# Products of ones in TensorE's order in the first layer, and a second plan of expert tiles that is made in steps

## The chip, the cores and the metric

The kernel runs on one core of a Trainium2 chip. A core has TensorE (PE) for matmuls, VectorE (DVE), ScalarE (ACT) and GpSimd (POOL) for everything else, and SyncE (SP), which here only starts transfers. Each engine works through its own list of instructions in order, and waits on semaphores where it needs another's result. The metric is the time of one execution on the device, in microseconds, as the median of several runs.

## What is computed

Four sequences of 256 tokens with 256 features pass through two layers. Cut to what matters:

```
x = x + L0_attention(layernorm(x))   # 16 heads of 16, each token sees the last 128 (and itself)
x = x + L0_ffn(layernorm(x))         # 1024 wide, ReLU, weights stored in 4 bits with a scale for 64,
                                     # plus a low-rank (LoRA) part
x = x + L1_scan(layernorm(x))        # selective state space, 16 states:
                                     #   h[l] = exp(dt*A)*h[l-1] + dt*B[l]*x[l];  y[l] = sum_n C[l,n]*h[l,n]
n = layernorm(x)
a = n + L1_attention(rmsnorm(n))     # 32 query heads of 128, 4 key/value heads, causal
x = x + a + MoE(rmsnorm(a))          # 32 experts, each token goes to its 8 best, and a shared expert
```

The experts are chosen by sigmoid scores with a bias, and weighted by the scores of the eight, normalised. Everything is float32.

## The kernel before

**First layer, a sequence at a time.** `l0_attention(b)` is a generator. It projects q, k and v, then for eight pairs of heads `l0_lowest` (matmul L360) makes raw scores `l_sc` with matmuls of 16 rows (the head's dimension), and DVE reduces each head's scores to the lowest value per query (custom operation at L367, output `l_junk` and a column of `qpad`). That column makes a 17th row of q, so that a second product, `l_sT` in `l0_softmax` (L381), comes out transposed and with the lowest score taken off already. ACT takes the exponential (L388), POOL masks it (L393, L397), and `l0_values` (L409) multiplies by v, with matmuls that fill 32 columns of the array for each head (`l_av`). After every eight heads `l0_divide` copies the sums (ACT, L418, `l_o`), spreads the denominators over the partitions with a matmul (`l_den`, L420), inverts them on DVE (L421) and multiplies (L422, `l_oT`). `l0_close` (L430) applies the output weights (`l_po`, 16 matmuls on all 128x128 of the array) and DVE adds the result to x (L434). `feed_forward` then makes the norm (`ff_ln`, `ff_xn`), transposes (`ff_pT`, L190), and runs `ff_pu` (L482, up) and `ff_pd` (L497, down). While sequence 0 is in `l0_lowest`, `dequantise` unpacks the 4-bit weights on DVE (L238, L241, L245, L250) and adds the low-rank product that PE makes (`lora_up`, L240; `lora_dn`, L249).

**Scan.** `scan(b)` works through 16 states. For each one, PE copies B and C to all partitions (`sm_pbc`, L561, bf16, 96 rows), ACT makes the decay (L568), DVE multiplies (L572), scans (L574) and multiplies again (L579, `sm_hc`), and POOL adds up `sm_y` (L581). At the end PE transposes `sm_y` (`sm_py`, L587) and DVE adds it to x (L590).

**Second layer.** The attention runs in pairs of query heads (queries L655, scores L677/L678, values L727, output `at_po` L737). During the opening, SP also fills the DRAM areas of the expert stage with zeros (`zeros()`, 36 transfers, L752). The expert stage sorts the tokens by expert into slots of DRAM: `route` (L860 on) scores the tokens of a sequence, finds each token's slots (`mo_tops` L908, `mo_at` L909) and POOL scatters the rows with indirect transfers (`slots`, L918). A plan says which expert and which slots each tile of 128 slots takes. `plan("early")` makes the first 16 tiles (EARLY) from the first three sequences' counts, and `plan("late")` all others once the last sequence is routed. In it `late_pc` (L785) is a matmul with the counts, then follow some 20 small steps on DVE (L791 to L826), three matmuls `late_pv` that spread the results (L831), and the copies out of them (L836 to L851). `experts` is a software pipeline over the tiles: load a tile (SP, L1215), transpose (`mx_pT`, L1225), gate and up (`mx_pgu`, L1233), weights and slots (`mx_wj`, `at`, DVE, L1248, L1253, L1255), activation (`mx_act`, L1263), turn and down (L1268 to L1278), copy out (`mx_o`, L1286) and add into DRAM with an indirect transfer of POOL (`sum`, L1287). 64 tiles (FEWEST) are always there; a Switch on a count that the late plan leaves (`arm`, L844) picks the program for the rest. At the end four partial sums are loaded and added to x (L1366, L1371, L1372).

**Order.** The streams are Python generators. `play` takes from the stream with the smallest mark, `timed` gives each stream its marks as pieces `(from, to, steps)`, and so the instructions get the order in which they are handed over; a scheduler may still move them, except in the last `play(streams)` and in the Switch, which stand in a manual schedule. The late plan is the stream `planned()` (L1331), which makes the whole plan in one step, at (6, 6, 2).

**PSUM.** `ps(name)` hands out a bank of 128x512 f32. Tag "w" has six banks that go round, "acc" two. Whoever gets a bank waits until all readers of its last owner are done.

Of the kernel before, what the change touches and what calls it, by code (L numbers as in the profile page):

```python
# [16 lines left out]
P = 128  # L17
# [35 lines left out]
def block_kernel(ctx: ExitStack, tc, out, a):  # L53
# [16 lines left out]
    def g2(name, dtype=F32):  # L70

        return gen.tile([P, 512], dtype, tag="g2", name=name)

    def halves(t):
        return t.rearrange("p (t d) -> p t d", t=2)
# [119 lines left out]
    def rows(b):  # L195

        return x[:, 2 * b : 2 * b + 2, :]
# [154 lines left out]
    def l0_lowest(b, u, seq):  # L352

        pair, j = l0_pair(u)
        qT, kT = seq["qT"], seq["kT"]
        scs = [ps(f"l0_sc{b}_{h}") for h, _ in pair]
        for q, cols in ((0, slice(0, P)), (1, slice(P, 3 * P))):
            for (h, r0), sc in zip(pair, scs):
                rows_ = slice(r0, r0 + HD0)
                T.matmul(  # L360
                    sc[:, cols], qT[rows_, j, q * P : (q + 1) * P],
                    kT[rows_, j, 0 : cols.stop - cols.start], start=True, stop=True,
                )
        for (h, _), sc in zip(pair, scs):
            junk = l0.tile([P, 3 * P], F32, tag="junk", name=f"l0_junk{b}_{h}", bufs=1)
            for t, cols, mask in ((0, slice(0, P), mask_first), (1, slice(P, 3 * P), mask_window)):
                V.tensor_tensor_reduce(  # L367
                    junk[:, cols], sc[:, cols], mask, 1.0, 3.0e38,
                    ALU.add, ALU.min, seq["pads"][t][:, h, HD0 : HD0 + 1],
                )  # L370
# [54 lines left out]
    def l0_close(b, seq):  # L425

        po = halves(ps(f"l0_po{b}"))
        for t in range(2):
            for j in range(4):
                T.matmul(  # L430
                    po[:, t, :], seq[j // 2][:, j % 2, t * P : (t + 1) * P], wo0[:, j, :],
                    start=j == 0, stop=j == 3,
                )
        V.tensor_tensor(rows(b), rows(b), po, ALU.add)  # L434

    def l0_attention(b):

# [68 lines left out]
    def scan(b):  # L506
# [50 lines left out]
        for n in range(NS):  # L557
            pbc = halves(ps(f"sm_pbc{b}_{n}"))
            for i in range(2):
                k = i * NS + n  # L560
                T.matmul(  # L561
                    pbc[:, i, :], sel[:, k : k + 1].to_broadcast([96, P]), bc,
                    start=True, stop=True,
                )

            da = decays[n % 3]
            for c in range(2):
                A.activation(  # L568
                    da[:, c, 1:], dt[:, c, 1:], AF.Exp, scale=na[:, c, n : n + 1]
                )  # L570
            w = sw.tile([P, 2, S], F32, tag="w", name=f"sm_w{b}_{n}")
            V.tensor_tensor(w, u, pbc[:, 0:1, :].to_broadcast([P, 2, S]), ALU.mult)  # L572
            hs = sw.tile([P, 2, S], F32, tag="hs", name=f"sm_h{b}_{n}")
            V.tensor_tensor_scan(  # L574
                hs.rearrange("p c l -> p (c l)"), da.rearrange("p c l -> p (c l)"),
                w.rearrange("p c l -> p (c l)"), 0.0, ALU.mult, ALU.add,
            )
            hc = y if n == 0 else sw.tile([P, 2, S], F32, tag="hc", name=f"sm_hc{b}_{n}", bufs=2)
            V.tensor_tensor(hc, hs, pbc[:, 1:2, :].to_broadcast([P, 2, S]), ALU.mult)  # L579
            if n > 0:  # L580
                G.tensor_tensor(y, y, hc, ALU.add)  # L581
            yield
        yield
        py = halves(ps(f"sm_py{b}"))
# [189 lines left out]
    def plan(nm, n, early):  # L774

        def small(name, n=NE, dtype=F32):
            return end[0].tile([P, n], dtype, tag=f"plan_{name}", name=f"{nm}_{name}", bufs=1)

        c16 = stat.tile([P, NE], BF16, tag="mo_chosen16", name=f"{nm}_c16", bufs=1)
        V.tensor_copy(c16, chosen)
        pc = ps(f"{nm}_pc")[:, 0:NE]

        T.matmul(pc, ones16, c16, start=True, stop=True)  # L785
        count, tiles, cum, junk = small("count"), small("tiles"), small("cum"), small("junk")
        ti = small("ti", dtype=I32)
        ex, one = small("ex", 1), small("one")
        total = small("total", 1)
        j, used, vals = small("j", 1), small("used", 1), small("vals", 3)  # L790
        V.tensor_copy(count, pc)  # L791
        V.tensor_scalar(ti, count, 0.0 if early else float(P - 1), None, ALU.add)
        V.tensor_scalar(ti, ti, 7, None, ALU.arith_shift_right)
        V.tensor_copy(tiles, ti)
        if not early:
            V.tensor_tensor(tiles, tiles, taken, ALU.subtract)
        V.tensor_tensor_scan(cum, ones_ne, tiles, 0.0, ALU.mult, ALU.add)
        V.tensor_copy(total, cum[:, NE - 1 :])
        V.tensor_scalar(junk, cum, part, None, ALU.is_le)
        V.tensor_reduce(ex, junk, AX.X, ALU.add)  # L800
        V.tensor_scalar(one, enum, ex, None, ALU.is_equal)
        V.tensor_tensor(cum, cum, tiles, ALU.subtract)
        if early:

            V.tensor_scalar(taken, cum, -1.0, float(EARLY), ALU.mult, ALU.add)
            V.tensor_scalar(taken, taken, 0.0, None, ALU.max)
            V.tensor_tensor(taken, taken, tiles, ALU.min)
        else:
            V.tensor_tensor(cum, cum, taken, ALU.subtract)

        V.tensor_tensor(junk, one, cum, ALU.mult)
        V.tensor_reduce(j, junk, AX.X, ALU.add)
        V.tensor_tensor(j, part, j, ALU.subtract)
        V.tensor_scalar(j, j, float(P), None, ALU.mult)
        if early:
            V.tensor_copy(vals[:, 1:2], ex)
            V.scalar_tensor_tensor(vals[:, 0:1], ex, float(CAP), j, ALU.mult, ALU.add)
        else:
            live = small("live", 1)
            V.tensor_tensor(junk, one, count, ALU.mult)  # L820
            V.tensor_reduce(used, junk, AX.X, ALU.add)
            V.tensor_scalar(live, ex, float(NE) - 0.5, None, ALU.is_lt)
            V.tensor_tensor(vals[:, 1:2], ex, live, ALU.mult)
            V.tensor_tensor(vals[:, 2:3], used, j, ALU.subtract)
            V.scalar_tensor_tensor(j, ex, float(CAP), j, ALU.mult, ALU.add)
            V.tensor_tensor(vals[:, 0:1], j, live, ALU.mult)  # L826

        rows_of = 2 if early else 3
        pv = ps(f"{nm}_pv")[:, 0 : rows_of * n].rearrange("p (q i) -> p q i", q=rows_of)
        for q in range(rows_of):  # L830
            T.matmul(  # L831
                pv[:, q, :], vals[:, q : q + 1].to_broadcast([P, P]), ident[:, 0:n],
                start=True, stop=True,
            )
        which = end[0].tile([P, n], F32, tag=f"{nm}_which", name=f"{nm}_which", bufs=1)
        V.tensor_copy(which, pv[:, 1, :])  # L836
        regs = end[0].tile([1, 2, n], I32, tag=f"{nm}_regs", name=f"{nm}_regs", bufs=1)
        V.tensor_copy(regs[:, 0, :], pv[0:1, 0, :])
        V.tensor_scalar(regs[:, 1, :], pv[0:1, 1, :], 2.0 * P, None, ALU.mult)
        if early:  # L840
            return regs, which, None, None, None

        arm = end[0].tile([1, 1], I32, tag="arm", name="arm", bufs=1)
        V.tensor_scalar(arm, total[0:1], float(EARLY - FEWEST), None, ALU.add)  # L844

        lo = end[0].tile([P, n], F32, tag="lo", name="lo", bufs=1)
        hi = end[0].tile([P, n], F32, tag="hi", name="hi", bufs=1)
        spare = small("spare", 1)
        V.tensor_scalar(spare, part, float(CAP), None, ALU.add)
        V.tensor_scalar(lo, pv[:, 2, :], part, spare, ALU.is_le, ALU.mult)  # L850
        V.tensor_scalar(hi, lo, float(CAP - 1), None, ALU.max)  # L851
        return regs, which, lo, hi, arm

    taken = stat.tile([P, NE], F32, tag="taken", name="taken", bufs=1)

# [4 lines left out]
    def route(b, row):  # L860
# [51 lines left out]
            )  # L912

        if b == B - 2:
            tables.append(plan("early", EARLY, True))
        for t in range(2):
            for k in range(TOPK):
                inst = G.indirect_dma_start(  # L918
# [58 lines left out]
    def timed(stream, *pieces):  # L977


        marks = [lo + (hi - lo) * i / n for lo, hi, n in pieces for i in range(n)]  # L980
        return [stream, marks, 0, False]
# [346 lines left out]
            yield  # L1328


    def planned():  # L1331
        yield
        tables.append(plan("late", LATE, False))
        yield

    under_way = ahead, {}, {}, {}, {}, {}, {}, {}
    streams = [
        timed(shared(), (-1, 3, 2), (10, 18, 4)),
        timed(experts(FEWEST, range(FEWEST), under_way), (-2, FEWEST - 2, FEWEST)),
        timed(planned(), (6, 6, 2)),  # L1340
    ]
    play([timed(last_route[0], (0, 3, 3), (3, 5, 9))], streams)
    with tc.manual_schedule():
# [137 lines left out]
```

## Time and profile before

| | us |
|---|---|
| median of 3 runs | 1109.64 (1108.83 to 1111.13) |
| the profiled execution | 1098.13 |
| its span, first to last instruction | 1096.4 |
| mean granted TensorE clock | 0.908 |
| PE busy | 932.8 (85%) |
| DVE busy | 727.3 (66%) |
| POOL busy | 510.1 (47%) |
| ACT busy | 491.1 (45%) |

The profiled execution is 11.5 us shorter than the median of the runs, so the two are not mixed: differences between stages are read within the profile, and only their sum is carried over to the median. The times in the texts are from the start of the span. PE's clock ("PEclk") is the share of full speed that the throttle granted; it takes two values, 0.50 and 1.00, and a figure between them is a mean. A line of the timeline gives the start, the duration, engine, line, operation, out<-in, the shape, how many instructions were merged, and in brackets the idle time ahead of them with what ended it. A line of the windows gives a stretch, its length, and for each engine the busy time with the number of instructions, then the clock, the share of the DMA engines that was busy, and what they moved in GB/s. An f32 matmul appears as two records, so that x8 in a line of l_sc is four products.

The page's chain of work that ended last names the indirect sums (5%) and waits of PE in the expert stage first; the rest of the span falls into many small pieces, so the stages are read one by one.

### The profile page before, as it was taken

To read this page: it belongs to the slowest core of one execution; us is meant where nothing else is said; L and a number is where in the kernel's file an instruction comes from. 1 tells how busy PE (TensorE), PEld (TensorE's weight loads), DVE (VectorE), ACT (ScalarE), POOL (GpSimd) and SP (SyncE) were. 2 spreads that over 40 slices of the span, in tenths; PEclk is the share of its full clock that TensorE was granted. 3 is DMA by queue.
4 is the path that set the end of the run, shared out by engine and by line. 5 is a ranking of instruction groups with operands and counts; after the bars stand their busy time and mean duration, and the time that the engine had idled before them with its cause. 6 is when DMAs were issued, how large, how long until landed. Compare 5 with 4: busy or idle time off the path is not lost. (4 is left out here: it accounts for less than half of the span.)

```text
span 1096.4 us, 15761 instructions
## 1 busy us (share of the span) xinstructions
PE 932.8 (85%) x4589; PEld 696.5 (64%) x4589; DVE 727.3 (66%) x2237; ACT 491.1 (45%) x1503; POOL 510.1 (47%) x534
## 2 busy tenths in 40 slices
PE   4898976478898999999899989899998997999770
PEld 2655743355666687767677766677877875777650
DVE  6746149947996775899686489896475536555454
ACT  2031233324655364656555466655564554444330
POOL 5030123413456332344865135775335624888781
PEclk9576776788898999999999989999999998999995
DMA  8985999960110111111222473223223327799867
GB/s 214 236 180 132 255 246 241 245 217 26 39 49 30 39 39 38 49 49 49 62 80 71 134 226 101 72 99 101 68 83 99 108 84 252 147 155 150 155 73 206
DMA packets 131716, 134.31 MB, mean 123 GB/s; under 512 B 10592, under 2 KB 125440, under 8 KB 131616
## 3 DMA queue, kind: packets, MB, share of 16 engines
q1 hardware_dynamic: 118032, 114.12, 39.0%
q0 software_dynamic: 13584, 19.05, 9.6%
q8 instruction: 40, 0.66, 0.3%
q14 instruction: 60, 0.49, 0.1%
HBM read 70.45 MB, written 62.69 MB: 121 GB/s over the span
## 5 line engine op out<-in xcount | busy, mean ns | idle before, releaser
L607 POOL TENSOR_TENSOR at_q_rot<-at_q_t,at_q_t 128x512 f32<-128x512 f32 x64 | 85.0, 1328 | 139.6 <-DVE at_q_t L603 116.8
L686 ACT ACTIVATE at_pr<-at_pr,at_low 128x128 f32<-128x128 f32 (+1 forms) x256 | 113.6, 445 | 52.0 <-DVE at_low L682 49.7
L737 PE MATMUL at_po<-at_wo,at_oT 128*128 128x256 f32 x512 | 129.6, 387 | 2.2 <-ACT at_oT L730 2.1
L655 PE MATMUL at_pq<-at_hT,at_wq 128*128 128x256 f32 x512 | 125.7, 389 | 3.1 <-DVE at_q_t L603 1.8
L696 POOL TENSOR_SCALAR at_pr<-at_pr,at_rden 128x128 f32<-128x128 f32 x128 | 87.8, 695 | 80.4 <-DVE at_rden L691 62.9
L1287 POOL DMA_INDIRECT sum<-mx_o,at x73 | 113.8, 1559 | 24.1 <-issue 9.4
L581 POOL TENSOR_TENSOR sm_y<-sm_y,sm_hc 128x512 f32<-128x512 f32 x60 | 77.2, 1287 | 86.0 <-DVE sm_hc L579 82.9
L655 PEld LDWEIGHTS at_pq<-at_hT,at_wq 128*128 128x128 f32 x512 | 98.0, 196 | 19.7 <-DVE at_q_t L603 2.0
L737 PEld LDWEIGHTS at_po<-at_wo,at_oT 128*128 128x128 f32 x512 | 95.4, 193 | 17.3 <-ACT at_oT L730 3.4
L603 DVE TENSOR_TENSOR at_q_t<-at_pq,rope 64x512 f32<-64x512 f32 x128 | 88.1, 688 | 15.4 <-POOL at_k_rot L607 12.9
L568 ACT ACTIVATE decay<-sm_dt,na 128x255 f32<-128x255 f32 x128 | 58.7, 500 | 64.4 <-DVE sm_h L574 58.4
L574 DVE TENSOR_TENSOR_SCAN sm_h<-decay,sm_w 128x512 f32<-128x512 f32 x64 | 84.5, 1320 | 1.3
L719 ACT COPY at_pT<-at_pa 128x512 f32<-128x512 f32 x64 | 37.2, 581 | 104.1 <-PE at_pa L712 104.0
L918 POOL DMA_INDIRECT slots<-mo_row,mo_at x64 | 64.4, 1007 | 39.0 <-DVE mo_at L909 21.1
L682 DVE CUSTOM_DVE_ANT_0 at_pr<-at_sc,masks 128x128 f32<-128x128 f32 (+1 forms) x256 | 78.4, 353 | 4.6 <-PE at_sc L678 3.0
L678 PE MATMUL at_sc<-at_k_rot,at_q_rot 128*128 128x256 f32 x256 | 76.5, 380 | 0.0
L727 PE MATMUL at_pav<-at_pT,at_v 128*128 128x512 f32 x128 | 67.4, 609 | 2.8 <-DVE sm_hc L579 1.3
L601 DVE TENSOR_TENSOR at_q_t<-at_pq,rope 128x512 f32<-128x512 f32 x64 | 43.8, 684 | 38.4 <-PE at_pq L655 38.0
L393 POOL TENSOR_SCALAR_AFFINE_SELECT l_pr<-l_pr 128x512 f32<-128x512 f32 x32 | 22.4, 700 | 97.7 <-ACT l_pr L388 97.7
L700 ACT ACTIVATE at_pr<-at_pr,at_rden 128x256 f32<-128x256 f32 x128 | 57.9, 501 | 8.2 <-DVE at_rden L691 8.0
L677 PEld LDWEIGHTS at_sc<-at_k_rot,at_q_rot 128*128 128x128 f32 x256 | 47.9, 190 | 12.7 <-issue 2.7
L1233 PE MATMUL bank<-wgu,mx_xT 128*128 x192 | 52.0, 394 | 3.9 <-DVE mx_act L1263 3.4
(357 smaller groups left out, 2038.9 us busy)
## 6 DMA issues: line engine op xcount, KB each, us to landing
slots<-zero SPq DMA_DIRECT2D x32, 1156.0 KB, 20.3
at_wq<-in_Wq_dram SPq DMA_DIRECT2D x64, 256.0 KB, 2.7
at_wo<-in_Wo_dram SPq DMA_DIRECT2D x64, 256.0 KB, 2.8
xg<-slots SPq DMA_DIRECT2D x73, 144.5 KB, 3.1
sum<-zero SPq DMA_DIRECT2D x4, 1152.0 KB, 12.7
wgu<-in_Wg_dram SPq DMA_DIRECT2D x32, 128.0 KB, 3.0
wgu<-in_Wu_dram SPq DMA_DIRECT2D x32, 128.0 KB, 3.3
wd<-in_Wd_dram SPq DMA_DIRECT2D x8, 512.0 KB, 6.7
```

Source lines behind the costliest of these rows:

```text
L574: V.tensor_tensor_scan(hs.rearrange("p c l -> p (c l)"), da.rearrange("p c l -> p (c l)"), w.rearrange("p c l -> p (c l)"), 0.0, ALU.mult, ...
L581: G.tensor_tensor(y, y, hc, ALU.add)
L603: V.tensor_tensor(t2[lo : lo + 64], src[hi : hi + 64], sin[hi : hi + 64].unsqueeze(1).to_broadcast([64, n, S]), ALU.mult,)
L607: G.tensor_tensor(dst, t1, t2, ALU.add)
L655: T.matmul(pq[:, i, :], wq[:, c, i * HD : (i + 1) * HD], hT[:, c, :], start=c == 0, stop=c == 1,)
L678: T.matmul(sc[:, P : 3 * P], qT[:, i, P:S], kT[:, 0, :], start=True, stop=True)
L682: V.tensor_tensor_reduce(pr[:, cols], sc[:, cols], mask, 1.0, 3.0e38, ALU.add, ALU.min, low[:, k : k + 1],)
L686: A.activation(pr[:, cols], pr[:, cols], AF.Exp, scale=-1.0, bias=low[:, k : k + 1], accum_out=den[:, k : k + 1],)
L696: scaled.append(G.tensor_scalar(prs[i][:, cols], prs[i][:, cols], rden[:, k : k + 1], None, ALU.mult).ins)
L727: T.matmul(pav, v_sb[:, 0, cols], pT[0], start=True, stop=False)
L737: T.matmul(po[:, t, :], oT[:, i, t * P : (t + 1) * P], wo[:, i, :], start=h0 + i == 0 and t == 0, stop=h0 + i == NH - 1 and t == 1, skip_g ...
L1287: G.indirect_dma_start(out=sums[i % SUMS], out_offset=bass.IndirectOffsetOnAxis(ap=at, axis=0), in_=o, in_offset=None, compute_op=ALU.add,)
```

## The change

A helper `warm(n)` takes a bank of the "w" set and issues n bf16 products of a 128x128 block of ones with 512 columns of ones; nobody reads the result. It is called with 2 after the scores of each pair of heads in `l0_lowest` of sequences 0 and 1 (16 calls), with 12 at the end of `l0_close` of sequence 0, and with 6 in each of the last three states of sequence 0's scan: 62 products in all. `plan` becomes a generator that yields between groups of its steps, and the late one is spread over marks 5 to 13 in 11 steps instead of being made at once at 6; the early one is still run through in one go.

```diff
+    def warm(n):
+        bank = ps("warm")
+        for _ in range(n):
+            T.matmul(
+                bank, ones16, ones16.unsqueeze(1).to_broadcast([P, 4, P]), start=True, stop=True
+            )
...
@@ l0_lowest, after the products l_sc of a pair
+        if b < 2:
+            warm(2)
...
@@ l0_close, after x's add
+        if b == 0:
+            warm(12)
...
@@ scan, at the end of a state
+            if b == 0 and n >= NS - 3:
+                warm(6)
...
@@ plan
         T.matmul(pc, ones16, c16, start=True, stop=True)
+        yield
...
         if not early:
             V.tensor_tensor(tiles, tiles, taken, ALU.subtract)
+        yield
         V.tensor_tensor_scan(cum, ones_ne, tiles, 0.0, ALU.mult, ALU.add)
         V.tensor_copy(total, cum[:, NE - 1 :])
+        yield
...
         V.tensor_scalar(one, enum, ex, None, ALU.is_equal)
+        yield
...
             V.tensor_tensor(cum, cum, taken, ALU.subtract)
+        yield
...
         V.tensor_scalar(j, j, float(P), None, ALU.mult)
+        yield
...
             V.tensor_tensor(vals[:, 0:1], j, live, ALU.mult)
+        yield
...
                 start=True, stop=True,
             )
+        yield
...
         if early:
-            return regs, which, None, None, None
+            tables.append((regs, which, None, None, None))
+            return
+        yield
...
         V.tensor_scalar(arm, total[0:1], float(EARLY - FEWEST), None, ALU.add)
+        yield
...
-        return regs, which, lo, hi, arm
+        tables.append((regs, which, lo, hi, arm))
...
         if b == B - 2:
-            tables.append(plan("early", EARLY, True))
+            for _ in plan("early", EARLY, True):
+                pass
...
-    def planned():
-        yield
-        tables.append(plan("late", LATE, False))
-        yield
...
-        timed(planned(), (6, 6, 2)),
+        timed(plan("late", LATE, False), (5, 13, 11)),
```

How the scheduled orders differ: POOL's list is the same, and SP's but for one zero-fill that goes out one place later. On PE the pairs of products of sequence 0 stand after the scores of their pair of heads. Those of sequence 1's first four pairs stand between the scores and the values of the first sequence's last heads, the fifth ahead of the first four records of `l_po`, the sixth after `pln`, the last two in the feed-forward. Of the twelve, eight stand between the first four records of `l_po` and the rest, four after it. The three groups of six follow `sm_pbc` of states 13, 14 and 15. On DVE, two dequantising steps that wait for `lora_dn` come one pair of heads later, the reductions of sequence 1's last two pairs stand amid the feed-forward's norm, and the late plan's steps stand in small groups between those of the tiles. `late_pc` follows the first tile's gate product, and `late_pv` comes three to four tiles later.

## The prediction

> **What bounds the kernel now.** I read the page's 40 slices first, because the change is spread over a few short stages.
>
> ```profile
> PE   4898976478898999999899989899998997999770
> POOL 5030123413456332344865135775335624888781
> PEclk9576776788898999999999989999999998999995
> ```
>
> A slice is 27.4 us. TensorE's clock is low only in the first eight slices (to 219 us) and in the last. From slice 10 to 33 PE is busy and at full clock (in 260 to 900 it is busy 599.30 of 640.00 us, clock 0.98): matmuls bound it, and a shift of its start moves its end. Then POOL takes over. The windows by stage show the beginning:
>
> ```profile
> core 0: us, PE busy (x) PEld busy (x) DVE busy (x) ACT busy (x) POOL busy (x), PEclk, DMA share, GB/s
> 27.30:64.80 37.50, 31.83 (x115) 20.97 (x114) 22.75 (x90) 3.71 (x10) 2.56 (x4) 0.50 1.00 236
> ...
> 85.30:88.70 3.40, 3.40 (x18) 2.10 (x17) 2.74 (x13) 0.87 (x2) 2.06 (x3) 0.50 0.00 0
> ...
> 105.80:109.20 3.40, 0.43 (x2) 0.03 (x1) 2.29 (x9) 0.41 (x2) 0.00 (x0) 1.00 1.10 215
> 109.20:112.60 3.40, 2.67 (x11) 1.79 (x12) 0.92 (x4) 0.59 (x1) 1.26 (x1) 0.50 1.08 302
> ```
>
> The clock changes on a grid of about 3.4 us (85.3, 102.4 and 109.2 lie on it). 105.8 to 109.2 is a stretch of 0.43 us of PE work, and the next is at 0.50. In 85.3 to 88.7 PE counts as busy throughout and the clock stays at 0.50; there it runs l_sc and l_sT, with 16 or 17 rows, and l_av, with 32 columns. So what raises the clock here is not busy time but work on the whole array. Weighting each matmul's columns streamed by the share of rows and columns it uses, grid windows at half clock with 0.77 or more were followed by full clock, those with 0.54 or less by half (between, both); at full clock those with 0.32 or less fell, those with 0.34 or more did not.
>
> PE's timeline shows what the half clock costs in the first sequence's close:
>
> ```profile
> 95.55 2.08 PE L420 MATMUL l_den<-l_o,spread 128*128 128x512 f32 x2 [0.69 <-ACT l_o L418]
> 97.55 1.65 PE L360 MATMUL l_sc<-l_kT,l_qT 16*128 16x128 f32 x8
> 99.13 2.08 PE L430 MATMUL l_po<-wo,l_oT 128*128 128x256 f32 x4
> 101.00 1.06 PE L1060 MATMUL pln<-ident,ln2c 128*128 128x128 f32 x4
> 101.99 1.45 PE L360 MATMUL l_sc<-l_kT,l_qT 16*128 16x128 f32 x8
> 103.37 2.86 PE L430 MATMUL l_po<-wo,l_oT 128*128 128x256 f32 x12
> 109.93 0.69 PE L190 MATMUL ff_pT<-ident,ff_xn 128*128 128x128 f32 x2 [3.70 <-DVE ff_xn L171]
> ```
>
> The first l_den, at full clock (81.21), took 1.12; this one 2.08. The chain is l_av, l_den, DVE's reciprocal (97.73, 3.36 us), l_po, x's add (106.27), the norm, ff_pT.
>
> At the end, POOL issues without a pause, 16 scatters from 914.37, then 73 sums of 1.56 us with 0.30 between:
>
> ```profile
> 914.37 1.03 POOL L918 DMA_INDIRECT slots<-mo_row,mo_at  x1 [21.09 <-DVE mo_at L909]
> ...
> 934.70 1.62 POOL L1287 DMA_INDIRECT sum<-mx_o,at  x1 [0.31 <-DVE at L1253]
> 936.63 1.59 POOL L1287 DMA_INDIRECT sum<-mx_o,at  x1 [0.30 <-issue]
> ```
>
> From 934.70 to 1072.3 is 137.6 us; 73 at 1.861 are 135.9. The slack is 1.7 us, nearly all at 1031 to 1035, at the Switch.
>
> **The plan in steps.** Before, PE waits 4.66 us for late_vals (915.2 to 919.85) while 28 small DVE steps (914.70 to 922.7) run in one piece. After, tiles' work stands between them. But all of it lies beside POOL's 16 scatters, which run to 934.4 whatever PE does, and the sum of the first late tile, the seventeenth, goes out 16 x 1.861 = 30 us after 934.70. Gain 0. Below: the 1.7 us, if tiles that run ahead also shorten the Switch. Above: late_c (0.17 us) now stands on DVE ahead of mo_tops and mo_at, for which POOL waited 21.09 us; with the first of late_count's steps between the two mo_at, 0.4 at most, since the second mo_at is due only eight scatters (10 us) on. POOL's own order is unchanged; SP's differs by one zero-fill, one place later. I take **0**, from -1.7 to +0.4.
>
> **A product of ones.** The trace has none. The nearest rows are sm_pbc, bf16 with 256 columns: at full clock two took 0.39 (205.50) and four 0.60 (202.35), so 0.105 each, 0.21 for 512 columns; 0.42 at half clock. Six at half took 1.46 (159.11), 0.49 per 512 columns at most. A pair: **0.85 at half, 0.43 at full**. Each group also takes one of the six "w" banks, whose next owner waits until the group is done, and waits itself until the bank's last reader is done.
>
> **Eight pairs in sequence 0's l0_lowest (32 to 52).** A pair of heads costs PE 1.65 at half clock and DVE about 1.6, plus 0.69 for each of the dequantising steps between. Both are nearly full, and the clock is 0.50 in all of it. With a pair of products PE needs 2.5 a pair, 8 x 0.85 = 6.8 in all. Against that: PE stood idle 0.86 and 0.43; DVE stood 1.00 and 2.12 for lora_dn (46.19, 54.12), and in the new order these two steps come behind one more pair of heads. Following the banks by hand, with half clock throughout, the last reduction goes from 56.5 to 59.3: +2.8. If PE ends up the only bound, +4.4. The products add 0.25 of an array's work to a window with one pair, which would lift that of 30.7 (0.55 to 0.80) and perhaps that of 47.8 (0.35 to 0.6 or more); a window at full clock gives back up to 1.7 each. Bounds 0 to +4.4; I take **+1.5**.
>
> **Sequence 1's first four pairs (82 to 95).** The window from 81.9 had 0.23 and fell. One pair at full clock adds 0.43 / 3.41 = 0.125: 0.36, just above the bound. While the next pair waits for DVE's reciprocal (to 85.7), little is added; from there a unit of l_sc, l_av and a pair, about 1.9 us long as DVE takes it, holds 0.43 + 0.1 + 0.19 = 0.72, that is 0.38: above by little. If the clock holds, DVE sets the pace: 85.7 + 0.7 + 8 heads x 0.79 = 92.7 in place of 94.9 (-2.2); l_den 1.12 for 2.08 (-1.0). l_po's rest was issued at 103.37 although l_oT was ready at 101.88; at full clock PE's work between, eight products (1.7) included, ends in time (-1.5). x's add is then **4.7 earlier**. If the clock falls, three pairs add 2.55 ahead of l_den, and eight products 1.7 to 3.4 ahead of l_po's rest, less what the window clock gives back there: x's add **3.0 later**.
>
> **The close and the feed-forward (106 to 123).** Four products, pln and the next l_sc with its pair now stand after l_po: 0.85 + 0.5 + 0.1 + 0.43 = 1.9 us of array work in the window that had 0.11, about 0.55, so the clock stays full even if it rose only at l_po. From ff_pT at 109.93 to the first ff_pd at 122.33 PE was bound at half clock (12.4 us). At full clock the same matmuls take about 6.5, two more pairs 0.86, and some 0.6 of ACT's copy shows: 8.0, **-4.4**. If it falls all the same, two pairs cost +1.7 there.
>
> **The scan's end (18 products).** By the banks, the groups wait for hc of states 9, 8 and 11 and run between 202 and 211, where PE is at full clock already; a state takes DVE 3.3 us and a group 1.3, so nothing is delayed. PE then stands still, as before, until sm_py at 223.70, which waits for POOL's sm_y: over 9 us, far more than the grid. ff_pu (3.62) stays at half. **0**, from -2 to +0.5.
>
> **Does a shift reach the end?** 122.9 to 143.3 is PE at full clock, 163.8 to 222.3 DVE (55.11 of 58.50 us), then PE. Zero-fills hold the queues until about 236, but the first weights of the attention that follow them are needed at 264.9: covers gains of this size. Where the grid falls in 143 to 164 (clock 0.67) can give or take 3.
>
> **Sum**: 0 + 1.5 - 4.7 - 4.4 + 0 = -7.6. The profiled execution would go from 1098.13 (span 1096.4) to 1090.5. It lies 11.5 us below the median of the runs, 1109.64; the same -7.6 gives **1102.0** there.
>
> The Trainium skill ("TensorE: Matmul & The Clock Gate", Part 1) says that the gate opens after about 3.4 us of a busy PE and closes after such an idle stretch. By busy time alone, the products in l0_lowest and in 85 to 95 would change nothing, since PE counts as busy there; only their cost would stay, and the sum would be that of the second rival. The rows above (busy 3.40 of 3.40, clock 0.50) speak against it.
>
> **Rivals.** (1) The change does not do what it says between 85 and 102: the margins are 0.36 and 0.38 against 0.33, and the clock falls as before, but holds through the feed-forward. 0 + 1.5 + 3.0 - 4.4 = +0.1: **1109.7**, give or take 3. (2) Slower: at half clock the products take PE's place and banks ahead of needed work, and the window after l_po falls as well. +2.8 + 3.0 + 1.7 = +7.5: **1117**. It decides wherever windows with products stay below about 0.6 at half clock, and where PE, not DVE, ends a pair in l0_lowest. For it: PE is full there. Against it: the 0.55 after l_po. (3) More: the clock also rises in 30 to 57 and the grid falls well in 143 to 164: l0_lowest 0, 57.7 to 64.8 at full clock -3, and -3 later: 0 - 3 - 4.7 - 4.4 - 3 = -15: **1094.5**.
>
> **Chances.** Forecast 0.45 (1099 to 1106), (1) 0.22, (2) 0.18, (3) 0.15. Range 1094 to 1116: half of (3) and a third of (2) lie outside, and a little of the rest. About 0.2% (2.2 us) is what this kernel's runs can tell from no change. Faster: 0.44 + 0.15 and 0.04 of (1), 0.63; same: 0.13; slower: 0.24.
>
> **What would show it.** Clock 1.00 in the window after 85 and from x's add to ff_pd; l_den's second at about 1.1 us; ff_pd first at about 115 from the span's start; l0_lowest's last reduction 0 to 3 us later; POOL's first sum about 20.3 us after its first scatter, as before. It is wrong if l_den stays at 2.08, if l_sT starts later than 60.5, or if POOL's sums show gaps other than those at the Switch.

## The result: slower by 0.85%

| | us |
|---|---|
| changed kernel, median of 11 runs | 1115.5 (1113.0 to 1122.51) |
| kernel before, median of 11 runs | 1109.02 (1105.5 to 1111.13) |
| ratio after / before | 1.0085, 95% interval 1.0066 to 1.0104 |
| profiled execution after (its span) | 1114.92 (1113.2) |

The forecast was 1102.0 us; the kernel went the other way, near the number of the second rival: 0.85% of 1109 are 9.4 us (7.3 to 11.5 by the interval; the two medians alone differ by 6.5), where that one had 7.5. The later runs were made in four sets, in which the kernel before has medians of 1107.2, 1106.9, 1100.2 and 1100.2 us. So each ratio is against before's own runs in the same set, on the same chip.

The two recorded profiles differ by 16.8 us, far more than the runs do. The profile of before was an untypical execution. A second one (e1_before, below) has a span of 1105.3 and is the better partner. Stage by stage, from the traces (each point is the start of the instruction unless it says end):

| stretch | before | e1_before | after | after less e1_before |
|---|---|---|---|---|
| start to the last reduction of l0_lowest, sequence 0 (end) | 56.52 | 56.45 | 60.76 | +4.3 |
| from there to the first reciprocal | 25.85 | 24.20 | 23.84 | -0.4 |
| first reciprocal to the second l_den's end | 15.25 | 14.52 | 18.91 | +4.4 |
| l_den's end to x's add | 8.64 | 11.22 | 9.24 | -2.0 |
| x's add to ff_pT | 3.66 | 3.66 | 4.52 | +0.9 |
| ff_pT to the first ff_pd | 12.40 | 12.40 | 8.90 | -3.5 |
| ff_pd to the scan's add to x | 102.52 | 102.16 | 101.76 | -0.4 |
| the scan's add to the first at_pq | 12.78 | 12.78 | 16.30 | +3.5 |
| first at_pq to close1 | 664.57 | 664.68 | 664.64 | 0.0 |
| close1 to the first scatter | 12.16 | 12.16 | 12.16 | 0.0 |
| first scatter to the first sum | 20.33 | 24.62 | 23.98 | -0.6 |
| first sum to the last | 136.02 | 140.08 | 141.26 | +1.2 |

Three stretches lose (4.3, 4.4, 3.5), and two win something back. The lines after, first PE in sequence 0's l0_lowest (start, duration, engine, line, operation, shapes, number of records):

```profile
39.22 1.03 PE L78 MATMUL warm<-ones 128*128 128x512 bf16 x2
40.19 1.77 PE L368 MATMUL l_sc<-l_kT,l_qT 16*128 16x128 f32 x8
41.89 1.03 PE L78 MATMUL warm<-ones 128*128 128x512 bf16 x2
```

A pair of heads takes 41.89 - 39.22 = 2.67 us of PE, one instruction right behind the other: PE is the bound here, at half clock, and the two products are 0.97 of it (40.19 - 39.22).

The windows of the changed kernel (start:end, length, busy time of PE, weight loads, DVE, ACT, POOL with instructions in brackets, clock, DMA share, GB/s):

```profile
27.30:64.80 37.50, 34.74 (x123) 18.00 (x123) 22.63 (x89) 2.76 (x6) 1.68 (x3) 0.50 0.99 238
85.00:88.40 3.40, 2.55 (x22) 1.38 (x20) 3.40 (x4) 0.87 (x2) 0.16 (x1) 1.00 0.01 2
88.40:91.80 3.40, 3.40 (x16) 1.55 (x16) 2.63 (x15) 0.30 (x1) 1.21 (x2) 0.50 0.01 2
...
108.90:112.30 3.40, 3.40 (x17) 2.64 (x16) 0.01 (x1) 0.00 (x0) 0.00 (x0) 1.00 1.08 252
112.30:115.70 3.40, 3.12 (x20) 1.64 (x19) 2.37 (x11) 0.78 (x3) 0.00 (x0) 1.00 1.09 297
115.70:119.20 3.50, 1.93 (x12) 1.21 (x12) 1.75 (x11) 0.58 (x1) 1.26 (x1) 0.99 1.09 247
119.20:122.60 3.40, 3.40 (x9) 2.49 (x9) 1.22 (x8) 0.00 (x0) 0.00 (x0) 0.51 1.09 235
```

The clock falls at 88.4, as the first reciprocal ends (87.96), and before it fell at 85.3 (85.73). It rises at 108.9 and stays over the gap behind x's add (112.75), which had lost it before, for three windows. PE's timeline of the close answers to the lines shown of before:

```profile
101.44 2.08 PE L430 MATMUL l_den<-l_o,spread 128*128 128x512 f32 x2 [0.69 <-ACT l_o L428]
103.45 1.65 PE L368 MATMUL l_sc<-l_kT,l_qT 16*128 16x128 f32 x8
105.03 1.03 PE L78 MATMUL warm<-ones 128*128 128x512 bf16 x2
105.86 1.91 PE L440 MATMUL l_po<-wo,l_oT 128*128 128x256 f32 x4
107.56 2.56 PE L78 MATMUL warm<-ones 128*128 128x512 bf16 x8
109.96 2.75 PE L440 MATMUL l_po<-wo,l_oT 128*128 128x256 f32 x12
112.55 1.03 PE L78 MATMUL warm<-ones 128*128 128x512 bf16 x4
```

l_den still takes 2.08, and eight products (2.4 us up to the next instruction) stand between the parts of l_po.

The third loss lies ahead of the attention. ACT in the changed kernel:

```profile
231.40 0.84 ACT L500 ACTIVATE ff_hT<-ff_pu,b_up 128x256 f32<-128x256 f32 x2 [15.18 <-PE ff_pu L494]
232.13 0.20 ACT L160 ACTIVATE at_ln_t<-at_ln_ve 128x2 f32<-128x2 f32 x1
```

and in the profile of before:

```profile
226.78 0.20 ACT L152 ACTIVATE at_ln_t<-at_ln_ve 128x2 f32<-128x2 f32 x1 [14.35 <-DVE at_ln_ve L168]
227.01 0.20 ACT L153 ACTIVATE at_ln_y<-at_ln_t 128x2 f32<-128x2 f32 x1
228.27 0.84 ACT L488 ACTIVATE ff_hT<-ff_pu,b_up 128x256 f32<-128x256 f32 x2 [1.05 <-PE ff_pu L482]
```

The norm's step on ACT now stands behind an ff_hT, which waits for PE's ff_pu. DVE's next step of the norm waits 2.78 us in place of 0.50. PE after the feed-forward's ff_pd:

```profile
236.86 0.70 PE L198 MATMUL at_pT<-ident,at_hn 128*128 128x128 f32 x4 [2.94 <-DVE at_hn L631]
238.12 5.40 PE L642 MATMUL at_pv<-wv,at_hT 128*128 128x512 f32 x8 [0.56 <-ACT at_hT L636]
```

It stands still for 2.94 us (1.25 before), the clock falls (0.50 from 238.6 to 242.0; before it is 1.00 there), and at_pv takes 5.40 in place of 3.70.

### The profile page after: what moved, and what is told of

It reads as the page before. It is cut to its first block, busy times and chain, and to the rows that moved or that the text cites. A ratio compares the mean times of both kernels' runs of the same rounds, so it can differ in the third digit from the quotient of the medians.

```text
span 1113.2 us, 15886 instructions
## 1 busy us (share of the span) xinstructions
PE 946.7 (85%) x4651; PEld 696.4 (63%) x4651; DVE 726.2 (65%) x2237; ACT 490.7 (44%) x1503; POOL 509.9 (46%) x534
## 4 chain that ended last, share of the span: by engine, by line
PE 43%; DVE 26%; DMA 7%; POOL 6%; issue 6%; SPq 5%; ACT 5%; another core or an unknown queue 1%; POOLq 0%; DVEq 0%; ACTq 0%
PE at_po L751 5%; PE at_pq L669 5%; DVE sm_h L586 4%; DVE at_q_t L617 4%; SPq L766 3%; PE at_pav L741 3%; DMA sum<-mx_o,at 2%; DVE sm_hc L591 2%; PE at_sc L692 2%; DVE sm_w L584 2%; DVE at_pr L696 2%; PE bank L1259 2%; DMA slots<-zero 2%; PE ff_pu L494 2%; POOL at_pr L710 2%
```

## The experiments

Theory A, formed from these traces: the products cost the time, by PE's time at half clock (sequence 0), by standing ahead of l_den and l_po while the clock falls all the same (sequence 1), and by the order that the scheduler makes around them (scan); the plan costs nothing. Theory B: the plan in steps is what costs, through a stall in the expert stage.

**e1_before**: the kernel before, nothing edited.

> The kernel before, unchanged, to see an execution of it that is nearer to its median than the one of 1098.13 us. Theory A (the products cost the time; the stall in which TensorE, VectorE and ScalarE stand still together from 931 to 944 us in the changed kernel's profile comes with the execution, not with the change): 1106 to 1111 us, and the profile shows such a stall of 8 to 13 us somewhere in the expert stage, so that the span is near 1107. Theory B (the stall belongs to the plan in steps): the profile again shows none, and the span is near 1097, or the time is lost elsewhere.

Measured: 1108.08 us, ratio 1.0007 (0.9979 to 1.0035), span 1105.3. At the first scatter it is within 0.2 us of the first profile (in between they differ by up to 2.5). Then DVE (start, duration, and in brackets the idle time ahead with what ended it):

```profile
937.30 0.35 DVE L1263 SCALAR_TENSOR_TENSOR mx_act<-mx_sg,mx_w,mx_pgu 128x128 f32<-128x128 f32 x1 [12.97 <-ACT mx_sg L1239]
```

and POOL:

```profile
933.33 0.96 POOL L918 DMA_INDIRECT slots<-mo_row,mo_at  x1 [0.30 <-issue]
938.85 1.62 POOL L1287 DMA_INDIRECT sum<-mx_o,at  x1 [4.56 <-DVE at L1253]
941.36 1.59 POOL L1287 DMA_INDIRECT sum<-mx_o,at  x1 [0.88 <-DVE at L1253]
945.03 1.56 POOL L1287 DMA_INDIRECT sum<-mx_o,at  x1 [2.08 <-DVE at L1253]
```

DVE stands still for 12.97 us. Against the usual pause of 0.30 the first sum loses 4.3 us, and the sums after it lose 3.2 more. The stall is in the changed kernel's profile too (DVE 13.24 us, ended at 943.70), so it is not the change's. It holds for A. These 7.4 us are most of the 8.9 by which the spans of the two profiles of before differ; 0.9 more lie at the Switch.

**e2_plan**: the changed kernel without the three calls of `warm`.

> The plan in steps alone, without products of ones. Theory A: as before, 1107 to 1111 us, late_pv without a wait of 4.66 us and the sums at their pace of 1.861 us. Theory B: the stall comes along, 1114 to 1120 us, with the start of the attention (the first at_pq) where it was, near 237.6 us.

1106.83 us, ratio 1.0001 (0.9976 to 1.0026). The first scatter comes 12.2 us after close1 as before, first scatter to first sum is 24.22, and late_pv stands behind the same stall (12.12 us on PE), not behind late_vals. The sums don't keep the pace of 1.861 us that A had, since the stall breaks it. The plan in steps is worth nothing either way that these runs can tell (0.25%). In this execution the feed-forward stretch took 9.49 in place of 12.40 with the same instructions up to there: the clock's grid fell otherwise. Theory B falls.

**e3_ones**: before, with all the products; the plan at once.

> The products of ones alone, the plan made at once as before. Theory A: the first at_pq 6.6 us later than before, as in the changed kernel, and 1115 to 1117 us. Theory B: the first at_pq 6.6 us later too, but the median no more than 2 to 4 us above that of before, since what the profile of before has ahead of the tail is given back by the clock; 1111 to 1113 us.

1117.39 us, ratio 1.0104 (1.0057 to 1.0151). The first at_pq is at 245.25, the stretches are those of the changed kernel within 0.4 us (60.85; 18.57; 9.62; 4.52; 8.95; 16.30). The products make all of the difference.

**e4_not_seq0**

```diff
-        if b < 2:
+        if b == 1:
             warm(2)
```

> The changed kernel without the eight pairs of products in sequence 0's l0_lowest (those of sequence 1, the twelve at the close, the eighteen at the scan's end and the plan in steps stay). Theory A: those pairs cost 5 us at half clock and bring nothing; without them x's add of l0_close comes at 105 to 108 us in place of 113 and the median is 1108 to 1112 us. Theory B: the pairs are not what costs; 1114 to 1117 us.

1111.02 us, ratio 1.0046 (1.0024 to 1.0069). l0_lowest's last reduction is back at 55.71, x's add at 107.67. Reciprocal to l_den's end stays at 18.86, the norm's stretch at 16.29. So the eight pairs of sequence 0 are about half of the loss.

**e5_no_scan**: e4_not_seq0, and without the products in the scan.

```diff
-            if b == 0 and n >= NS - 3:
-                warm(6)
```

> The changed kernel without the pairs in sequence 0's l0_lowest and without the eighteen products at the scan's end; the pairs of sequence 1, the twelve at the close and the plan in steps stay. On ScalarE the norm ahead of the attention (at_ln_t, at_ln_y) stands ahead of the third ff_hT again. Theory A (the scan's products cost 3.5 us by putting ff_hT ahead of the norm on ScalarE, and nothing by their own time): the first at_pq comes 3.5 us earlier after x's add of the scan than in e4_not_seq0, near 235.5 us, and the median is 1106 to 1109. Theory B (the 3.5 us are the luck of the clock's grid): the first at_pq stays at about 239, median 1110 to 1112.

1110.23 us, ratio 1.0024 (0.9987 to 1.0062): the time says neither. The profile does: scan's add to first at_pq is 12.78, as before, in place of 16.29. The attention behind it took 667.66 in place of 664.8 in this execution, which hides it. The same 3 us more stand in e7, e9, e10, e11, e12 and e14, with and without products near. In these seven traces alone, the clock is at half for three windows more: about 305 and 592 us behind the first at_pq, and once between close1 and the first scatter, which then takes 13.85 us in place of 12.16. The first of them in e9_close_only, and the window at the same distance in e1_before:

```profile
538.70:542.10 3.40, 3.40 (x13) 2.17 (x14) 1.91 (x2) 3.25 (x9) 2.93 (x4) 0.50 0.02 5
542.40:545.80 3.40, 3.14 (x15) 2.00 (x14) 1.65 (x3) 2.51 (x7) 2.92 (x4) 1.00 0.13 44
```

Just ahead of it PE waits 2.33 us for at_q_t in e9_close_only and 1.55 in e1_before; why it waits longer was not found.

**e6_scan_only**: before, with the eighteen products in the scan alone.

> The eighteen products at the scan's end alone, everything else as before; ScalarE has the third ff_hT ahead of the norm. Theory A: nothing moves up to the scan's end, at_ln_t waits for ff_hT (some 2.3 us), at_pv runs partly at half clock (some 1.2 us more); the first at_pq near 241 us and 1110 to 1112 us. Theory B: the products themselves do no harm; the first at_pq within 1 us of 237.6 and 1106 to 1109 us.

1108.2 us, ratio 1.001 (0.9969 to 1.0051), undecided by time. The profile has A's mechanism: ff_hT ahead of at_ln_t, and 16.29 us from the scan's add to at_pq. The start of at_pq (235.18) was 6 us earlier than A had it, since the feed-forward's add came at 132.07 by the clock's luck (ff_pT to ff_pd 8.25). In the 17 traces the norm's stretch is 16.29 or 16.30 in the four with products in the scan, and 12.68 to 12.79 in the thirteen without: +3.5 is theirs.

**e7_seq0_only**: before, with `if b == 0: warm(2)` in l0_lowest alone.

> The eight pairs of products in sequence 0's l0_lowest alone. Theory A (at half clock a pair takes 0.85 us of TensorE, which is the bound there): the last reduction 4 to 5 us later than before (60.5 to 61.5 in place of 56.5), the clock 0.50 throughout up to 64, and 1110 to 1113 us. Theory B (VectorE sets the pace, the products lie beside it): the last reduction within 1 us of 56.5, 1106 to 1109 us.

1111.78 us, ratio 1.0045 (1.001 to 1.0081). The last reduction comes at 59.30, +2.9; the window from 30 to 38 had a mean clock of 0.71, so one grid window was open here, which it is not in the changed kernel (+4.3). From the first l_sc to the last reduction it takes 27.41 us here, 28.76 in the changed kernel, and 24.46 to 24.48 in the eleven profiles without products there. A, a little smaller than A had it.

**e8_seq0_banks**: the same with products of 4 columns.

```diff
-                bank, ones16, ones16.unsqueeze(1).to_broadcast([P, 4, P]), start=True, stop=True
+                bank[:, 0:4], ones16, ones16[:, 0:4], start=True, stop=True
```

> As e7_seq0_only, but each product has 4 columns in place of 512: the banks turn as there, and TensorE's time for a pair is next to nothing. Theory A (TensorE's time is the cost): the last reduction within 1.5 us of before, 56 to 58, and 1106 to 1110 us. Rival (the turn of the banks is the cost, since a group holds one of six and TensorE runs less far ahead): the last reduction as late as in e7_seq0_only, 60 to 62, and 1110 to 1113 us.

1106.01 us, ratio 0.9982 (0.9946 to 1.0018). The last reduction comes at 57.85. From the first l_sc it takes 26.27 us, 1.8 more than without products. A pair of these still takes PE 0.27 us (39.17 to 39.44), so the turn of the banks and the order have 1.8 us at most; the rest, 1.1 in e7 and 2.5 in the changed kernel, is left to PE's time. So A has the larger part, and whether the rival has any of the 1.8 was not tried.

**e12_seq0_eight**: e7 with eight products in place of two.

> Eight products in place of two after each pair of heads of sequence 0 alone, to see what raises the clock. Theory A (the work on the whole array, weighted by rows and columns, counts): at half clock a pair of heads then takes 3.4 + 1.65 us with a weight of about 0.7, the clock goes to 1.00 within two or three pairs and stays, a pair then takes 1.7 + 0.9 us, and the last reduction comes at 57 to 63 us, no later than with two. Rival (the clock does not follow that weight): 0.50 throughout, a pair takes 5 us, the last reduction at 72 us or later.

One execution, 1104.19 us beside a median of 1100.17 of before; its time decides nothing. The windows do. From 38 to 46 us, first in e12_seq0_eight:

```profile
38.00:46.00 8.00, 8.00 (x48) 3.61 (x47) 7.11 (x29) 0.00 (x0) 0.00 (x0) 1.00 0.96 299
```

and in the changed kernel, with two products a pair:

```profile
38.00:46.00 8.00, 8.00 (x30) 3.60 (x28) 5.30 (x22) 0.00 (x0) 0.00 (x0) 0.50 1.01 278
```

PE is "busy" for 8.00 of 8.00 in both; what differs is how much of the array the matmuls use, and the clock. In e12 PE runs:

```profile
41.11 0.92 PE L368 MATMUL l_sc<-l_kT,l_qT 16*128 16x128 f32 x8
41.97 1.90 PE L78 MATMUL warm<-ones 128*128 128x512 bf16 x8
```

A pair of heads with eight products at full clock takes 2.69 us (41.11 to 43.80), no more than with two at half clock (2.67). The last reduction comes at 55.96, against 60.76 with two, and as early as in the kernels with no products there (55.38 to 56.61); from the first l_sc it takes 24.14 us. But that is one position of the grid. In e15_add_eight, with the same products here, the clock opened only at 43 us:

```profile
33.00:43.00 10.00, 10.00 (x33) 3.70 (x34) 5.58 (x21) 0.23 (x1) 0.00 (x0) 0.50 0.72 221
```

There the stretch takes 28.79 us, as long as with two products (28.76). What was won in e12 did not last either: lora_dn stands behind the products, the second w_dn starts at 57.86 (54.05 without) and l_sT at 59.52 (57.65).

**e9_close_only**: before, with `warm(12)` in l0_close(0) alone.

> The twelve products at the close alone; eight of them stand ahead of the rest of l_po, four behind. Theory A (they cost TensorE's time ahead of l_po and give it back in the feed-forward, where the clock now stays full, while without them it is open there in about half of the executions): x's add 1 to 3 us later after l_den's end than the 8.65 us of the profile of before; from ff_pT to ff_pd 8 to 9 us; the feed-forward's x add within 3 us of 138.0, and 1104 to 1109 us. Rival (the forecast's own step: the twelve are the strong part, worth 4.4 us and more): the feed-forward's x add 4 to 6 us earlier, 1101 to 1104 us.

1099.16 us, ratio 0.9982 (0.9962 to 1.0002). l_den's end to x's add 10.01 (8.64 and 11.22 in the two profiles of before), ff_pT to ff_pd 9.51, the feed-forward's add 134.01. That is 4 us ahead of 138.0, as the rival has it. But e8 (133.50) and e6 (132.07) have this add as early with none of these products, so the profile shows no gain of theirs. Here only two of the twelve stand behind l_po, and the clock is lost in the gap all the same (0.50 from 108.6 to 115.4). By time, no more than 0.4% can have been won, and it may be none.

**e10_seq1_only**: before, with `if b == 1: warm(2)` alone.

> The eight pairs of sequence 1 alone. Theory A (they don't hold the clock over VectorE's reciprocal, and three pairs at half clock stand ahead of l_den): clock 0.50 from about 85 to 102, from the first reciprocal to l_den's end 17 to 19 us in place of 14.5 to 15.3, 1107 to 1111 us. Rival (they hold the clock there when the others are absent): clock 1.00 from 82 on, from the reciprocal to l_den's end 12 us, 1101 to 1105 us.

1101.74 us, ratio 1.0011 (0.9989 to 1.0034). The clock is 0.50 from 85 on, reciprocal to l_den's end 18.59. That is A's mechanism. A's time, 1107 to 1111, was set where before had 1107; beside this set's 1100.17 the pairs cost 0.3% at most, and perhaps nothing.

**e13_seq1_six**: six in place of two for sequence 1's first four pairs (`if b == 1 and u < 4: warm(6)`), nothing else.

> Six products in place of two after each of sequence 1's first four pairs of heads, nothing else. Theory A (the clock fell over the reciprocal only because two products weigh too little; the grid window there had 0.24 with them, four more add 0.25): clock 1.00 from 81 to x's add, l_den's second 1.1 us in place of 2.08, from the first reciprocal to l_den's end 11 to 12.5 us in place of 14.5 to 18.6, 1097 to 1100 us on a chip where before has 1100. Rival (the banks and VectorE hold the pairs so far apart that some window still falls): 0.50 from 85 or 88 on, three groups at half clock cost 7.5 us ahead of l_den, 1105 us or more.

Windows of e13_seq1_six:

```profile
82.00:86.00 4.00, 3.66 (x29) 2.03 (x26) 3.19 (x15) 0.87 (x2) 0.99 (x2) 1.00 1.06 210
86.00:90.00 4.00, 4.00 (x36) 2.02 (x34) 1.83 (x12) 0.87 (x2) 0.99 (x2) 1.00 0.26 69
```

and of e10_seq1_only, with two:

```profile
82.00:86.00 4.00, 3.15 (x22) 1.75 (x22) 3.65 (x10) 0.87 (x2) 1.37 (x2) 0.85 0.01 3
86.00:90.00 4.00, 4.00 (x25) 2.17 (x22) 1.29 (x8) 0.87 (x2) 0.99 (x2) 0.50 0.01 2
```

With six the clock holds, and l_den is at full clock:

```profile
93.41 1.12 PE L430 MATMUL l_den<-l_o,spread 128*128 128x512 f32 x2 [0.69 <-ACT l_o L428]
```

x's add comes at 101.74, 4.5 to 4.7 us earlier than in the two profiles of before: the step that the forecast had, at its size. Part of that can be the grid's, since e6, without these products, has it at 104.73. But reciprocal to l_den's end is 15.23, not the 11 to 12.5 expected, since 24 products take 4 x 1.4 us of PE there; the gain lies in l_po's stretch (7.21). The median is 1098.39, ratio 0.9982 (0.9959 to 1.0006): hardly any of it is left in the typical execution. The profiled one, with a span of 1089.6, is the fastest of its ten (1091.45 to 1101.82), so the profile tells what can happen, not what mostly does.

**e11_after_add**: before, with products that the data puts behind x's add.

```diff
         V.tensor_tensor(rows(b), rows(b), po, ALU.add)
+        if b == 0:
+            bank = halves(ps("warm"))
+            for i in range(6):
+                T.matmul(bank[:, i % 2, :], ident, rows(b)[:, i % 2, :], start=True, stop=True)
```

> A version that may beat both: before, with six unread products of the identity with the new x of sequence 0 (f32, 256 columns) in l0_close. They read what x's add writes, so they can stand only behind it, where TensorE waits for the norm; pln and the next l_sc come behind them. Theory A (the clock is lost in that gap, and work put there by its data costs nothing ahead of l_po): clock 1.00 from x's add on, from ff_pT to ff_pd 7.5 to 9 us in place of 9.5 to 12.4, x's add 0 to 1.5 us earlier, the feed-forward's x add 3 to 6 us earlier than 138.0, 1102 to 1106 us. Rival (what is won there is lost in the clock's grid further on or to the wait of the scan): 1106 to 1109 us.

**1092.5 us, ratio 0.9924 (0.9901 to 0.9947)**, faster than both kernels. PE:

```profile
99.21 5.49 PE L430 MATMUL l_po<-wo,l_oT 128*128 128x256 f32 x12 [0.73 <-DVE l_oT L422]
105.47 2.86 PE L438 MATMUL warm<-x,ident 128*128 128x256 f32 x12 [0.78 <-DVE x L434]
108.17 0.61 PE L1064 MATMUL pln<-ident,ln2c 128*128 128x128 f32 x4
108.70 0.92 PE L360 MATMUL l_sc<-l_kT,l_qT 16*128 16x128 f32 x8
109.56 0.66 PE L190 MATMUL ff_pT<-ident,ff_xn 128*128 128x128 f32 x4
```

The products fill the gap of 3.70 us in which PE had waited for the norm, and the clock stays open:

```profile
105.10:108.40 3.30, 2.93 (x15) 2.62 (x16) 2.59 (x12) 0.41 (x2) 0.00 (x0) 1.00 1.12 183
108.40:111.80 3.40, 3.40 (x28) 2.37 (x27) 2.11 (x13) 0.96 (x2) 1.27 (x1) 1.00 1.06 286
```

pln and l_sc moved behind l_po and the products by themselves; what that is worth alone was not tried. They hold ff_pT up by 0.9 us (its input is ready at 108.67), so that x's add to ff_pT takes 4.83 in place of 3.66. From ff_pT to ff_pd it now takes 6.05 (12.40 in both profiles of before), less than the 7.5 expected. The profiled execution (1096.84 us) is the slowest of the twelve, with the three half-clock windows of e5.

**e14_add_six** is e11 with e13's products.

> e11_after_add and e13_seq1_six together. Theory A: both gains add up, x's add 2 to 5 us earlier than in e11_after_add and the feed-forward still at full clock; 1.0 to 1.4% below before. Rival (only the work behind x's add pays): no better than e11_after_add, 0.6 to 0.9% below before, or worse where the clock falls.

1090.19 us, ratio 0.9935 (0.9900 to 0.9969): no better than e11 alone as far as these runs can tell, as the rival has it. x's add comes at 103.16, 1.6 us earlier than in e11, where A had 2 to 5.

**e15_add_eight** is e11 with e12's products.

> e11_after_add and e12_seq0_eight together. Theory A (with the clock open from 33 on, l_sT and what follows up to 64 run at full clock, but lora_dn waits behind the products): the first reciprocal 0 to 2 us earlier than in e11_after_add, 0.7 to 1.0% below before. Rival (the products only pay their own cost there): 0.5 to 0.8% below before.

1092.18 us, ratio 0.9946 (0.9921 to 0.9971). The rival: the first reciprocal is at 83.51, 3 us later than in e11, since the clock opened only at 43 us here.

By time alone, the pairs of sequence 0 are the only single part that is shown to cost something (e7); the others cost 0.46% together (e4). What the pairs of sequence 1 and the products in the scan cost one by one rests on the profiles. Measured one by one, the parts add up to 0.5% (0.45 + 0.11 + 0.10 - 0.18) of the 0.85%, which their intervals allow.

## Why the prediction was wrong, point by point

- **The plan in steps, 0**: right (1.0001, interval of 0.25% on either side), and for the reason given: POOL's scatters start as long after close1, and the sums don't wait for the late plan. But the picture "POOL issues without a pause" was that of one untypical execution. (The small DVE steps in that stretch are 31, not 28, which changes nothing.)
- **A product of ones, 0.42 and 0.21**: 0.48 in pairs at half clock (0.97 for two), 0.24 at full (1.41 for six, from 80.06 to 81.45 in e13). Some 13% too low; of no weight.
- **Sequence 0's l0_lowest, +1.5 of 0 to +4.4**: mis-sized; +4.3, the upper end. The step that failed is "a window at full clock gives back up to 1.7 each": in the changed kernel no window opened. By the prediction's own weighting the window from 30.4 had 0.74, near the 0.80 worked out for it, and stayed at half; those from 33.8 to 54.3 had 0.36 to 0.43. The +2.8 that had been followed through the banks, and the +4.4 for PE as the only bound, were the better numbers; with PE at 2.67 a pair against DVE's 2.3, PE was the bound.
- **Sequence 1's first four pairs, -4.7**: the largest failure, of the sign. "0.36, just above the bound" took the window's weight of 0.23 from one position of the grid. In the changed kernel the window from 85.0 holds 0.24 with a pair in it. The price of the other case was +3.0; x's add came 6.4 us later than in e1_before, 4.3 of which l0_lowest had brought, so +2.1. e13 shows that the mechanism is there and the number of products was too small. Nor was 0.36 a safe margin: weighted in the same way, windows at full clock with 0.30 to 0.38 went either way in the 17 traces (up to 250 us).
- **The close and the feed-forward, -4.4**: right in mechanism, 3.5 in size. But half clock there is itself a matter of the grid: without products behind x's add, the same instructions took 12.40 in four executions, 9.49 and 9.50 in two, 8.25 in two. A gain against the first figure is not a gain against the median.
- **The scan's end, 0**: wrong by +3.5. The products' own time was indeed hidden, and the bound of +0.5 was drawn from it alone. What was overlooked is ACT's order, in which at_ln_t and ff_hT changed places; the list of changed orders has PE, DVE, POOL and SP only, and the swap was not priced. at_ln_t then waits for sm_py, ff_pu and ff_hT. That is the wait that a moved instruction brings for those queued behind it on its own engine.
- **The sum**: against e1_before at the first at_pq, +6.8 in place of -7.6. The 14.4 between them: l0_lowest 2.8 (4.3 for 1.5), from its end to ff_pT 7.6 (+2.9 for -4.7), the feed-forward 0.9 (-3.5 for -4.4), the scan's end 3.5, less 0.4 between.
- **The base**: the sum was made against a profile 11.5 us below the median, and the difference was carried along as if it lay outside the stages. The second profile of before is 8.9 us longer than the first, and 8.4 of these lie in the expert stage, from the first scatter to the last sum.
- **The second rival's 1117** is near the result partly by luck. L0_lowest and the first four pairs cost much as it said (4.3 and 2.1, for 2.8 and 3.0). But the window after l_po did not fall (-3.5 for its +1.7), and the scan's end, which it had at 0, cost 3.5.
- **The signs of being wrong** all came: l_den stayed at 2.08, l_sT started at 62.06, and POOL's sums have other gaps than those at the Switch (3.96 us ahead of the first). The last is the stall, and not the change's.
- The rule that the prediction cites (the Trainium skill, "TensorE: Matmul & The Clock Gate", Part 1, a gate that follows how busy PE is) would have led to the right sign, but these runs don't bear it out if PE's busy time in the profile is meant: with PE busy 8.00 of 8.00 us the clock was 0.50 with two products a pair and 1.00 with eight.

## What to carry to other kernels

In this kernel, filling work to hold the clock paid only where the engine was idle anyway and where it was enough to hold the clock; tie it to that gap by its data, since the scheduler here put most of the work without inputs ahead of what was needed. When an edit adds instructions on one engine, compare the order on all the others too: here one swap on ACT cost 3.5 us, where the added products themselves cost nothing. And take a second profile of the kernel before when its time is a per cent off the median.

## What the runs showed of the hardware that was not expected

- **The clock's grid is a lottery of some us.** The same instructions between ff_pT and ff_pd took 12.40, 9.49, 9.50 or 8.25 us, by where windows of about 3.4 us fell, and the three windows in the second layer that are at half clock in some executions go with 4.7 us more (3.0 in the attention, 1.7 behind close1). The times of e14 fit that: four lie at 1089.8 to 1090.2, three at 1094.9 to 1095.0, and the one profile, 1094.87, has the three windows. By the weight that the prediction works with, the windows over the reciprocal had 0.47 to 0.53 with six products a pair and stayed open; with two the first had 0.24 and fell. From half clock there is no sharp bound: the 17 traces (up to 250 us) have windows that rose from 0.57 up, and others that stayed at half with up to 0.74. So the weight says which way a window tends, and not what one near the bounds will do.
- **A stall of 13 us in the expert stage** (DVE 12.97 in e1_before, 13.24 in the changed kernel), in which PE, ACT and DVE do little while POOL issues its scatters, and which ends about 3 us after the last of them. It is in all profiles of e1 to e8 and after (first scatter to first sum 23.98 to 24.62), and in none of e9 to e15 or the first of before (20.28 to 20.37), which, but for that first profile, go with the lower medians of before (1100 against 1107 us). Kernels of one set share it, and one chip had it in one set and not in another. So it isn't the kernel's. What holds the engines the traces don't show, and it was not tried.
